# Cross-attention and a 4-bit-quantized FFN on one core: attention steps reordered, late scale guards, norm and splits re-placed

## The chip, the cores and the metric

The kernel runs on one core of a Trainium2 chip. A core has five engines that run their own instruction streams and meet through semaphores: PE (TensorE: matrix products and transposes), DVE (VectorE), ACT (ScalarE), POOL (GpSimd) and SP (SyncE, which here only issues DMAs). Times are device microseconds of one execution, the median of three runs for a kernel as a whole; the profile comes from one further execution. The granted clock is the share of full speed that PE was given.

## The reference

For 8 sequences of 128 rows of 512 values, cut to what is computed:

```python
x = x + xattn(layernorm(x), ctx, ctx, mask, Wq, Wk, Wv, Wo)
x = x + ffn(layernorm(x), w1, w2, w3)

# xattn: 32 query heads, 8 key/value heads of 128, rotary positions on q and k
logits = 30 * tanh(einsum(q, k) * 0.0884 / 30)
weights = softmax(where(mask, logits, -1e30))
attn = einsum(weights, v).reshape(b, t, 4096) @ Wo

# ffn: each of w1, w2 (1376 x 512), w3 (512 x 1376) goes through NF4:
# per 64 neighbours: absmax; w/absmax to the nearest of 16 codes; times absmax
h = silu(x @ dq1.T) * (x @ dq2.T)
out = h @ dq3.T
```

The mask is one 128 x 128 table for all sequences. The quantization of w1, w2, w3 is part of the computation.

## The kernel before

**Precision.** Each large product is taken as three PE products: both operands are split into a high half (rounded by an ACT copy) and a low half (source minus high, on DVE or POOL), and `product` adds high x low, high x high and low x high (L164 to L166). `split` is L150 and L151. So each product operand is preceded by an ACT instruction and a DVE or POOL instruction.

**Order.** The program switches on a manual schedule: each engine executes its instructions in the order in which the code issues them, and an instruction that must wait holds up all that is behind it on its engine. PSUM buffers are named by tags: "q" (two banks), "s" (one), "wo" (one), "pv" (two banks wide, one buffer), "c" (two banks wide, the quantizer's sum).

**Head** (first 118 us). A list of tiles, key, value and query projections, is walked; `plan[n]` holds what is to be issued beside tile n. `masks` turns the mask with PE (pm) and counts its valid keys with an all-ones product (pa). `scales` finds each block's absmax a, guards it against zero (r = max(a, 2^-126)) and inverts it, all on DVE. `Scales.turn` transposes a and r with PE (pt_ar), copies them out of PSUM on ACT (art, L310), and writes them to DRAM, from where they are read back broadcast (s_w).

**Quantizer.** `quantize` is a generator that goes through units of at most 128 x 1024 weights. A unit is multiplied by its inverse scales on POOL (w_w, L200), then 15 bounds follow, each an ACT instruction (nm_w, L190) and a DVE instruction (nc_w, L196, in PSUM), then it is multiplied by its scales and split by `store` (dqt or w3t). `pump(n)` advances it by about n bounds' worth; the calls of `pump` between other work set where quantization stands in the queues of ACT, DVE and POOL.

**Attention** (118 to about 600 us). 64 steps, one per (half of the batches x key/value head, batch). A step issues: `project` (output product of three steps ago, then acc += po on DVE), `store`, `turn` (transposes the attention output of two steps ago into aT, split by ACT and DVE), `end_store`, `pump`, `q_proj` (query product for the next unit of 4 steps, and the start of its rotation by `rope`: copies on ACT, rc_q on DVE, rs_q on POOL), `values` (weights x values of the last step, then 1/rowsum and ad on DVE), `scores` (logits pl on PE, tanh and exp on ACT, times mask on POOL), the rotation's last add (L447: on DVE for the first two units, on POOL later), and `pump`. `due` says in which step wo and wq weights are split.

**Norm and FFN.** From step 59 the second layer norm starts, two batches at a time: `LayerNorm.sums`, `finish` (1/sqrt by an integer guess and three refinements, `rsqrt`, L100 to L105, on DVE), `rows`. Then `gate_up` makes 22 pairs of products (pg, pu); a later call makes silu(pg) on ACT and hT = that x pu on DVE. `order` holds 20 of them, in a loop with `pump(3.45)`. The down product (pd) needs hT split into `hs` by `split_h`; three are split at the end of the loop, and one more in each iteration of the loop over `down`. Six batches' pd are kept in PSUM, batches 6 and 7 get theirs at the end.

## Time and profile before

| | |
|---|---|
| Median of three runs | 804.36 us (803.58 to 804.71) |
| Profiled execution | 806.1 us, its span 804.3 us |
| Mean granted clock | 0.994 |
| Busy: PE, DVE, ACT, POOL | 784.1, 640.2, 581.0, 462.0 us |
| PE waits over 2 us in all | po for acc 3.2 (3 times), po for aT 2.5 (twice), pd's first 2.4 (once) |
| DMA | 102.44 MB, mean 127 GB/s |

The span runs from the first to the last recorded instruction; the execution's own time has a little around it. Busy time counts an engine's instructions; PE's instructions overlap their neighbours slightly, so that a full PE reads as 97 to 100%. A wait row reads: engine, what waited, its line, what it waited for, then total, number and longest in us. Names are the program's with the numbers left out (po_17 is po).

### The profile page before, as it was taken

The numbers are of one execution on the slowest core, as the hardware profiler recorded it, in microseconds if no ns is written. First come the engines' busy times: TensorE is split into PE (matmuls) and PEld (weight loads), VectorE is DVE, ScalarE is ACT, GpSimd is POOL, SyncE is SP. The second block draws the span as 40 slices with busy tenths as digits, with TensorE's granted clock in tenths as the row PEclk, the third lists the DMA queues.
The fourth block names the chain that finished last, engine by engine and source line by source line (L and its number), as shares of the span: only waits on it lengthen the run. The fifth ranks groups of instructions, "written<-read, shape, count | busy, mean of one in ns | idle before, by whom it ended". The sixth has DMA issues, their size and how long they took to land.

```text
span 804.3 us, 11142 instructions
## 1 busy us (share of the span) xinstructions
PE 784.1 (97%) x3737; PEld 629.7 (78%) x3737; DVE 640.2 (80%) x875; ACT 581.0 (72%) x821; POOL 462.0 (57%) x370
## 2 busy tenths in 40 slices
PE   8899998999999999999999999999989999998998
PEld 6688876877877787787887878878768888886877
DVE  6747789889779797988898878888867788879941
ACT  6348767888887879798797979888522769759720
POOL 3469546687877778777787877877530322322100
PEclk9999999999999999999999999999999999998999
DMA  7856736435263616336164415330240335441011
GB/s 232 286 172 209 209 124 193 110 115 182 55 190 112 196 40 198 96 102 209 54 200 126 125 34 181 104 131 35 96 151 8 114 123 162 124 148 41 1 66 40
DMA packets 72167, 102.44 MB, mean 127 GB/s; under 512 B 6542, under 2 KB 41678, under 8 KB 72110
## 3 DMA queue, kind: packets, MB, share of 16 engines
q1 hardware_dynamic: 68942, 90.19, 36.3%
q0 software_dynamic: 3168, 11.54, 4.5%
q8 instruction: 30, 0.49, 0.3%
q14 instruction: 27, 0.22, 0.1%
HBM read 79.32 MB, written 22.38 MB: 126 GB/s over the span
## 4 chain that ended last, share of the span: by engine, by line
PE 82%; DVE 7%; issue 3%; DMA 3%; ACT 3%; POOL 1%; SPq 1%; DVEq 0%; POOLq 0%; ACTq 0%
PE po L166 7%; PE po L164 7%; PE po L165 7%; PE pq L164 7%; PE pq L166 6%; PE pq L165 6%; PE pv L659 6%; PE pl L646 6%; PE pt_a L157 3%; PE pd L166 3%; PE pd L164 3%; PE pd L165 3%; PE pvp L166 2%; PE pvp L164 2%; PE pvp L165 2%
## 5 line engine op out<-in xcount | busy, mean ns | idle before, releaser
L196 DVE SCALAR_TENSOR_TENSOR nc_w<-nm_w,nc_w 128x1024 f32<-128x1024 bf16 (+1 forms) x238 | 284.2, 1194 | 63.3 <-ACT nm_w L190 51.4
L190 ACT ACTIVATE nm_w<-w_w,bias 128x1024 bf16<-128x1024 f32 (+1 forms) x255 | 275.4, 1115 | 23.6 <-POOL w_w L200 19.2
L164 PE MATMUL po<-wo,aT 128*128 128x512 f32 x256 | 124.9, 488 | 3.2 <-DVE acc L673 3.2
L446 POOL TENSOR_TENSOR rs_q<-rs_q,sgnq 128x512 f32<-128x512 f32 x64 | 84.1, 1315 | 72.7 <-ACT rs_q L444 69.9
L652 POOL TENSOR_TENSOR th<-th,mt 128x512 f32<-128x512 f32 x64 | 83.6, 1306 | 43.0 <-ACT th L650 27.0
L164 PE MATMUL pq<-xT,wq 128*128 128x512 f32 x256 | 106.0, 414 | 0.3 <-DVE rc_q L445 0.3
L166 PE MATMUL po<-wo,aT 128*128 128x512 f32 x256 | 101.5, 397 | 2.5 <-DVE aT L151 2.5
L165 PE MATMUL po<-wo,aT 128*128 128x512 f32 x256 | 100.4, 392 | 0.0
L166 PE MATMUL pq<-xT,wq 128*128 128x512 f32 x256 | 100.2, 391 | 0.0
L165 PE MATMUL pq<-xT,wq 128*128 128x512 f32 x256 | 99.8, 390 | 0.0
L447 POOL TENSOR_TENSOR qr<-rc_q,rs_q 128x512 f32<-128x512 f32 x56 | 72.5, 1295 | 0.4 <-DVE rs L661 0.4
L659 PEld LDWEIGHTS pv<-vt,th 128*128 128x128 f32 x512 | 66.4, 191 | 4.9 <-POOL th L652 0.6
L164 PEld LDWEIGHTS po<-wo,aT 128*128 128x128 f32 x256 | 48.5, 190 | 27.4 <-issue 12.7
L659 PE MATMUL pv<-vt,th 128*128 128x129 f32 x512 | 67.6, 275 | 0.2 <-POOL th L652 0.2
L165 PEld LDWEIGHTS po<-wo,aT 128*128 128x128 f32 x256 | 48.7, 190 | 22.1 <-issue 13.8
L646 PE MATMUL pl<-qr,krt 128*128 128x512 f32 x128 | 65.6, 594 | 0.0
L443 ACT COPY rs_q<-pq 64x512 f32<-64x512 f32 x64 | 37.3, 582 | 38.9 <-PE pq L166 36.1
L200 POOL TENSOR_TENSOR w_w<-w_w,s_w 128x1024 f32<-128x1024 f32 (+1 forms) x17 | 39.8, 2343 | 43.1 <-DMA s_w<-scale_d 43.0
L649 ACT ACTIVATE th<-pl 128x512 f32<-128x512 f32 x64 | 38.4, 599 | 33.7 <-PE pl L646 33.2
L166 PEld LDWEIGHTS po<-wo,aT 128*128 128x128 f32 x256 | 48.4, 189 | 14.8 <-DVE aT L151 3.8
L166 PEld LDWEIGHTS pq<-xT,wq 128*128 128x128 f32 x256 | 48.0, 188 | 10.8
L164 PEld LDWEIGHTS pq<-xT,wq 128*128 128x128 f32 x256 | 48.2, 188 | 9.7 <-DVE rc_q L445 1.4
(141 smaller groups left out, 1710.0 us busy)
## 6 DMA issues: line engine op xcount, KB each, us to landing
s_w<-scale_d SPq DMA_DIRECT2D x60, 256.0 KB
w12t_d<-dqt SPq DMA_DIRECT2D x22, 512.0 KB
w<-w12t_d POOLq DMA_DIRECT2D x22, 512.0 KB, 4.5
raw_wq<-in_L_xattn_Wq SPq DMA_DIRECT2D x32, 256.0 KB
raw_wo<-in_L_xattn_Wo SPq DMA_DIRECT2D x32, 256.0 KB
ws<-in_L_ffn_w SPq DMA_DIRECT2D x20, 256.0 KB
w_w<-in_w12t SPq DMA_DIRECT2D x10, 512.0 KB
kr_d<-kr SPq DMA_DIRECT2D x16, 256.0 KB
```

The source lines that it names most:

```text
L164: E.matmul(out, ah, bl, start=start and i == 0, stop=False)
L165: E.matmul(out, ah, bh, start=False, stop=False)
L166: E.matmul(out, al, bh, start=False, stop=stop and i == n - 1)
L190: S.activation(m, self.w, AF.Relu, bias=bias[:self.p, i:i + 1], scale=BIG if up else -BIG)
L196: V.scalar_tensor_tensor(self.c, m, step, self.c, ALU.min, ALU.subtract if i == POS[0] else ALU.add)
L200: Q.tensor_tensor(self.w, self.w, self.s, ALU.mult)
L446: Q.tensor_tensor(s, s, every(sgn), ALU.mult)
L447: return lambda: (engine or Q).tensor_tensor(dst, c, s, ALU.add)
L646: E.matmul(pl, krt[kv, u % 2][:, bb * T:(bb + 1) * T], qr[u][:, bb].rearrange("p g t -> p (g t)"), start=True, stop=True)
L649: S.activation(th, pl, AF.Tanh, scale=ATTN_MULT / CAP)
L652: Q.tensor_tensor(em[i], em[i], mt.unsqueeze(1).to_broadcast([P, G, T]), ALU.mult)
L659: E.matmul(pv[:, g, :HD + 1], em[i][:, g], vt[kv][:, b], start=True, stop=True)
```

## The change

All parts keep the same arithmetic on the same data, and the same number of PE instructions (3,737 records before).

- `scales`: the guard goes from DVE to POOL, and the reciprocal becomes a later call: one tile later in the head, at the next bound in the quantizer. The scale turn is listed only after it. In the head, `store` begins at tile 9 instead of 6.
- `masks` is called at tile 6 and leaves its two PE steps and what hangs on them (`turn`, `count`) to tiles 10 and 12.
- Rotation: the second unit's last add goes to POOL; only the first unit's stays on DVE. With the new order it is issued before `values` and `scores` of its step, so ahead of that step's mask on POOL.
- Attention steps: the query product is issued first, then a pump (1.5; 1 in steps 0 and 1; none from 60), then projection, `turn` (step 2 no longer apart), then the rotation's last add, values, scores, and a pump of 1.65 instead of 2.15. One wo split moves from step 1 to step 2.
- Norm: for the first four batches the refinements of `finish` run on POOL, as four instructions each instead of three on DVE. The normalized rows 0 and 1 are made in step 61, rows 2 and 3 after the last step.
- Inner values: one split in each of the last four iterations of the gate_up loop instead of three in the last; the splits of batches 6 and 7 for the first two groups go to a separate buffer (`hs_67`), and are issued in the down loop from i = 2.
- Last banks: pd of batch 7 is made in two halves in different banks ("q" and "s"); before, both were halves of one bank.
- A small tile (`apart_2`) shifts addresses in the last pool.

```diff
...
 
-    def rsqrt(v, y, n, name):
+    def rsqrt(v, y, n, name, E=V):
         i = tp.tile([P, n], I32, tag="rs_i", name=f"i_{name}")
...
         for _ in range(3):
-            V.tensor_tensor(t, y, y, ALU.mult)
-            V.scalar_tensor_tensor(t, t, -0.5, v, ALU.mult, ALU.mult)
-            V.scalar_tensor_tensor(y, t, 1.5, y, ALU.add, ALU.mult)
+            E.tensor_tensor(t, y, y, ALU.mult)
+            if E is V:
+                E.scalar_tensor_tensor(t, t, -0.5, v, ALU.mult, ALU.mult)
+                E.scalar_tensor_tensor(y, t, 1.5, y, ALU.add, ALU.mult)
+            else:
+                E.tensor_tensor(t, t, v, ALU.mult)
+                E.tensor_scalar(t, t, -0.5, 1.5, ALU.mult, ALU.add)
+                E.tensor_tensor(y, y, t, ALU.mult)
 
...
 
-        def finish(self, apart=False):
+        def finish(self, engine=V, apart=False):
             n = len(self.bs)
...
             V.tensor_single_scalar(v, self.mv[:, :, 1], EPS, op=ALU.add)
-            rsqrt(v, self.y, n, self.name)
+            rsqrt(v, self.y, n, self.name, engine)
 
...
         V.tensor_reduce(a, blocks(w), AX.X, ALU.max, apply_absolute_value=True)
-        V.tensor_single_scalar(r, a, 2.0 ** -126, op=ALU.max)
-        V.reciprocal(r, r)
+        Q.tensor_single_scalar(r, a, 2.0 ** -126, op=ALU.max)
+        return lambda: V.reciprocal(r, r)
 
...
             self.s = nf.tile([P, 2, 16], F32, tag="nf_ar", name=f"ar_{self.h}")
-            scales(self.s[:, 0], self.s[:, 1], self.w)
-            fresh.append(self.turn)
+            last = scales(self.s[:, 0], self.s[:, 1], self.w)
+
+            def later():
+                last()
+                fresh.append(self.turn)
+            return later
 
...
             own = slice(self.cols.start // BLK, self.cols.stop // BLK)
-            scales(self.s[:, 0, own], self.s[:, 1, own], self.w)
-            if self.cols.stop == 4 * H:
-                fresh.append(self.turn)
+            last = scales(self.s[:, 0, own], self.s[:, 1, own], self.w)
+
+            def later():
+                last()
+                if self.cols.stop == 4 * H:
+                    fresh.append(self.turn)
+            return later
 
...
     def quantize():
+        invert = None
         for i, u in enumerate(units):
...
                 u.bound(b)
+                if invert:
+                    invert()
+                    invert = None
                 for when, s in found.get(i, ()):
...
                         yield 1
-                        s.find()
+                        invert = s.find()
                 if k == 2:
...
             product(pq, [((w[:, 0, k], w[:, 1, k]), (t[:, 0, k], t[:, 1, k])) for k in range(KT)])
-            return lambda: rope(qr[u][:, :, g, :], pq, cosq, sgnq, f"q{u}_{g}", V if u < 2 else None)
+            return lambda: rope(qr[u][:, :, g, :], pq, cosq, sgnq, f"q{u}_{g}", V if u < 1 else None)
 
...
                 Q.memset(ones, 1.0)
-                pm = bank("s", "pm")
-                E.transpose(pm[:, :T], mf, ident)
-                V.tensor_copy(mt, pm[:, :T])
-                pa = bank("s", "pa")
-                E.matmul(pa[:, :T], ones, mt, start=True, stop=True)
                 some = tp.tile([P, T], F32, tag="t_some", name="some", bufs=1)
-                V.tensor_single_scalar(some, pa[:, :T], 1.0, op=ALU.min)
-                V.tensor_tensor(cosq, tab[:, 0], some, ALU.mult)
-                V.tensor_tensor(sgnq, tab[:, 1], some, ALU.mult)
-                V.tensor_scalar(some, some, -1.0, 1.0, ALU.mult, ALU.add)
-                V.tensor_tensor(mt, mt, some, ALU.max)
+
+                def turn():
+                    pm = bank("s", "pm")
+                    E.transpose(pm[:, :T], mf, ident)
+                    V.tensor_copy(mt, pm[:, :T])
+
+                def count():
+                    pa = bank("s", "pa")
+                    E.matmul(pa[:, :T], ones, mt, start=True, stop=True)
+                    V.tensor_single_scalar(some, pa[:, :T], 1.0, op=ALU.min)
+                    V.tensor_tensor(cosq, tab[:, 0], some, ALU.mult)
+                    V.tensor_tensor(sgnq, tab[:, 1], some, ALU.mult)
+                    V.tensor_scalar(some, some, -1.0, 1.0, ALU.mult, ALU.add)
+                    V.tensor_tensor(mt, mt, some, ALU.max)
+                steps.extend([turn, count])
 
...
             plan[4] += [both[1].load]
-            plan[6] += [both[0].find]
-            plan[8] += [both[1].find]
+            inverts = []
+            plan[6] += [lambda: inverts.append(both[0].find())]
+            plan[7] += [lambda: inverts.pop()()]
+            plan[8] += [lambda: inverts.append(both[1].find())]
+            plan[9] += [lambda: inverts.pop()()]
             plan[12] += [units[0].load]
...
                 plan[20 + 2 * b].append(lambda b=b: turned[b]())
-            plan[8].append(masks)
+            steps = []
+            plan[6].append(masks)
+            plan[10].append(lambda: steps.pop(0)())
+            plan[12].append(lambda: steps.pop(0)())
             plan[15].append(lambda: ln.finish(apart=True))
...
                     f()
-                if 6 <= n < 19:
+                if 9 <= n < 19:
                     store()
...
 
-        due = {0: [("o", 0, 0)], 1: [("o", 0, 1), ("o", 0, 2), ("o", 0, 3)]}
+        due = {0: [("o", 0, 0)], 1: [("o", 0, 1), ("o", 0, 2)], 2: [("o", 0, 3)]}
         xn = {}
...
                 due.setdefault(i + (2 if i < 4 else 1), []).append(("q" if s8 < 4 else "o", kv + 1, s8 % 4))
+            tiles = {0: (0, 1), 1: (2,), 2: (3,), 3: ()}.get(i, (bb,)) if u + 1 < 2 * NKV else ()
+            later = [q_proj(u + 1, g) for g in tiles]
+            later = [f() for f in later]
+            pump(1.5 if 2 < i < 60 else 1 if i in (0, 1) else 0)
             if 0 <= i - 3:
...
                 ln.sums(i - 59)
+            if i == 61:
+                xn.update({k: pair.rows(k, "xn") for k in (0, 1)})
             store()
-            if 0 <= i - 2 and i > 2:
+            if 0 <= i - 2:
                 turn(i - 2)
             end_store()
-            if i < 60 and i != 2:
-                pump(1)
-            later = [q_proj(u + 1, g)() for g in ({0: (0, 1), 1: (2,), 2: (3,), 3: ()}.get(i, (bb,)))
-                      if u + 1 < 2 * NKV]
-            if i == 2:
-                turn(0)
+            for f in later:
+                f()
             if 0 <= i - 1:
...
             scores(i)
-            for f in later:
-                f()
-            pump(2.15 if 2 < i < 59 else 0)
+            pump(1.65 if 2 < i < 59 else 0)
             if i == 62:
...
             if i in (60, 62):
-                ln.finish()
-                xn.update({k: ln.rows(k, ("xn", "t2")[k // 2]) for k in (i - 60, i - 59)})
+                ln.finish(Q)
+                pair = ln
             for k in due.pop(i, ()):
...
 
+        xn.update({k: pair.rows(k, "t2") for k in (2, 3)})
         project(N - 3)
...
     f1 = ctx.enter_context(tc.tile_pool(name="f1", bufs=2))
+
+    f1.tile([P, 32], F32, name="apart_2", bufs=1)
     w3t, hs = {}, {}
 
+    last_hs, last_at = [(6, 0), (6, 1), (7, 0), (7, 1)], []
+
     def split_h(b, i):
         n = min(4, NHT - 4 * i)
-        t = hs[b, i] = wp.tile([P, 2, KT, P], F32R, tag="wq", name=f"hs_{b}_{i}", bufs=6)
+        if (b, i) in last_hs:
+            w = last_hs.index((b, i))
+            if not last_at:
+                last_at.append(wide("hs_67"))
+            t = hs[b, i] = last_at[0][:, :, :, w * P:(w + 1) * P]
+        else:
+            t = hs[b, i] = wp.tile([P, 2, KT, P], F32R, tag="wq", name=f"hs_{b}_{i}", bufs=6)
         split(t[:, 0, :n], t[:, 1, :n], hT[b // 4, i][:, :, b % 4 * T:b % 4 * T + T], V)
...
     down = most + [(b, 2) for b in range(6)] + [(b, i) for b in range(6, B) for i in range(3)]
-    to_split = list(down)
+    to_split = [k for k in down if k not in last_hs]
     last = len(order) - 1
...
             load_w12(w12_at[n])
-        if n == last:
-            for _ in range(3):
-                split_h(*to_split.pop(0))
+        if n >= last - 3:
+            split_h(*to_split.pop(0))
     evac()
...
             split_h(*to_split.pop(0))
+        if i == 2 and b < 4:
+            split_h(*last_hs[b])
         mine = pairs.setdefault(b, [])
...
             o = f1.tile([P, D], F32, tag="o", name=f"o_{b}", bufs=4)
-            if b >= 6:
-                pd.append(bank("q", f"pd_{b}"))
             parts = 2 if b == B - 1 else 1
...
                 own = slice(j * D // parts, (j + 1) * D // parts)
-                product(pd[b][:, own], [(s, (th[:, own], tl[:, own])) for s, (th, tl) in mine], start=b >= 6)
-                V.tensor_tensor(o[:, own], acc[b][:, own], pd[b][:, own], ALU.add)
+                to = pd[b] if b < 6 else bank(("q", "q", "s")[b - 6 + j], f"pd_{b}_{j}")
+                product(to[:, own], [(s, (th[:, own], tl[:, own])) for s, (th, tl) in mine], start=b >= 6)
+                V.tensor_tensor(o[:, own], acc[b][:, own], to[:, own], ALU.add)
                 nc.sync.dma_start(out[b][:, own], o[:, own])
```

## The prediction

> **What bounds the kernel now.** The profiled execution took 806.1 us with a span of 804.3; the runs' median is 804.36. I sum against the span and carry the difference over to the median unchanged. I read the page first, then PE's waits, then the waits in the timeline, then windows.
>
> ```profile
> PE 784.1 (97%) x3737; PEld 629.7 (78%) x3737; DVE 640.2 (80%) x875; ACT 581.0 (72%) x821; POOL 462.0 (57%) x370
> PE   8899998999999999999999999999989999998998
> PEclk9999999999999999999999999999999999998999
> PE 82%; DVE 7%; issue 3%; DMA 3%; ACT 3%; POOL 1%; SPq 1%; DVEq 0%; POOLq 0%; ACTq 0%
> ```
>
> PE is the bound: 97% busy, and 82% of the chain that ended last. From 250 to 350 us it is busy 100.00 of 100.00. There a step issues query product (12 matmuls at .227 us from start to start: 2.73), projection (2.73), four transposes (.44), eight value matmuls (.89) and logits (.86); that makes 7.65, and steps follow each other every 7.69. So no order of these can shorten a steady step: only PE's stalls and its low clock are to be had. I subtract those nominal spacings from the elapsed time: 34.5 us are lost in the whole span, 9.9 by 40 us, only 4.4 between 260 and 600 (2.3 to 573), and 10.1 after 730. The waits view names them:
>
> ```profile
> PE po L164 <- DVE acc L673: 3.2, 3, 1.5
> PE po L166 <- DVE aT L151: 2.5, 2, 1.7
> PE pd L164 <- issue: 2.4, 1, 2.4
> PE pd L166 <- DVE hs L151: 1.2, 1, 1.2
> PE pm L532 <- DVE mf L528: 0.9, 1, 0.9
> PE pt_ar L306 <- DVE ar L173: 0.7, 1, 0.7
> PE pa L535 <- DVE mt L533: 0.5, 1, 0.5
> PE pv L659 <- POOL th L652: 0.2, 1, 0.2
> ```
>
> (total, times, longest.) In windows (length, busy time of PE, PEld, DVE, ACT, POOL; then the granted clock) the clock follows a thin stretch:
>
> ```profile
> 130.40:133.90 3.50, 1.79 (x9) 0.87 (x7) 3.50 (x6) 2.52 (x5) 2.32 (x2) 1.00 0.69 209
> 581.00:584.40 3.40, 1.80 (x6) 0.57 (x6) 3.26 (x9) 1.23 (x2) 1.00 (x1) 1.00 0.00 0
> 584.40:587.80 3.40, 3.40 (x9) 2.62 (x10) 0.62 (x1) 0.00 (x0) 1.47 (x3) 0.51 0.50 139
> 731.20:734.60 3.40, 0.71 (x2) 0.30 (x2) 3.19 (x4) 3.40 (x6) 0.00 (x0) 1.00 0.27 88
> 734.60:738.00 3.40, 2.68 (x6) 2.15 (x7) 3.40 (x6) 3.40 (x6) 1.25 (x1) 0.50 0.07 28
> 738.00:741.40 3.40, 3.40 (x9) 2.64 (x8) 3.30 (x4) 2.98 (x4) 0.03 (x1) 0.50 0.11 36
> ```
>
> **1. Head, 30 to 37 us: -2.1 (-1.2 to -2.7).** The reciprocal moves one tile after its guard, the store of the first scale turn from tile 6 to 9, the mask's two PE steps to tiles 10 and 12. The waits of pt_ar, pm and pa (.7+.9+.5 in the view, 2.7 with the restarts in my account) lose their cause: their sources are then a tile (2.7 us) old. New: a scale turn lands directly after pm in the same bank and waits for a DVE copy, about .5. The two moved scale stores on SP stand just ahead of the loads that read them; a landing that is late there delays only the first quantization product on POOL. Late POOL work has about 3.5 us of slack here (the low halves of the last value weights end at 74.25 and are needed at 77.8).
>
> **2. Seam, steps 0 to 3: +3.5 (+1.5 to +5).** The final add of the second unit's rotated queries goes from DVE to POOL, ahead of step 0's mask; ACT gets one nm_w and one dqt copy ahead of step 0's tanh.
>
> ```profile
> 121.42 1.30 POOL L446 TENSOR_TENSOR rs_q<-rs_q,sgnq 128x512 f32<-128x512 f32 x1 [0.80 <-ACT rs_q L444]
> 122.72 1.71 POOL L652 TENSOR_TENSOR th<-th,mt 128x512 f32<-128x512 f32 x1
> 123.05 0.61 ACT L150 CAST dqt<-w_w 128x512 fp32r<-128x512 f32 x1
> 124.48 1.16 PE L659 MATMUL pv<-vt,th 128*128 128x129 f32 x8 [0.22 <-POOL th L652]
> ```
>
> Now the mask follows rs_q at once. In the new order POOL first has the dqt low half, which needs the ACT copy (ends near 123.1): 1.72 (its duration here), two adds and the mask at 1.30: 128.7, against 124.43. So the value matmuls, ready at 124.10, stall 4.65 instead of .38. PE's later stalls here (aT low half 1.92, .25, .27) have time to dissolve: 4.27-2.44 = +1.8. Then the clock. The Trainium skill, "TensorE: Matmul & The Clock Gate", Part 1, says that one idle window of about 3.4 us brings half clock; a 4.65 us stall covers a whole free-running window in (4.65-3.41)/3.41 = 36% of phases: .36 x 1.7 = +.6. The rows differ: 581.0 to 584.4 was only 1.6 idle, and the next window ran at .51; yet the similar 130.4 to 133.9 was not punished. A stall of 4.65 leaves some window with at least 2.3 idle, so I take one half-clock window, 3.4/2 = 1.7; ends 0 and 3.4.
>
> **3. Steady steps, 0 (±1), and the bubble at 246, -1.2.** Query product first, transposes directly before values, and pump shares 1.5/1.65 for 1/2.15: no PE work changes. acc, aT and ad get their readers later or at equal distance; laid out with the groups' mean durations, aT's low half ends 7.7 to 8.9 after its step's start and is due at 10.9, ad at 9.7 and is due at 13.15. The bubble is one event:
>
> ```profile
> 242.84 2.40 POOL L200 TENSOR_TENSOR w_w<-w_w,s_w 128x1024 f32<-128x1024 f32 x1
> 243.72 1.56 DVE L172 TENSOR_SCALAR ar<-ar 128x16 f32<-128x16 f32 x1
> 574.51 0.60 PE L157 MATMUL pt_a<-ident,ad 128*128 128x128 f32 x4
> 575.14 0.58 ACT L150 CAST aT<-pt_a 128x512 fp32r<-128x512 f32 x1 [1.94 <-PE pt_a L157]
> 575.88 1.12 PE L646 MATMUL pl<-qr,krt 128*128 128x512 f32 x2
> ```
>
> The scale guard, .17 to .45 elsewhere, took 1.56 on DVE until POOL's long product ended, acc came late and PE lost 1.25 in all. On POOL the guard can only queue behind that product, with nobody but the later reciprocal waiting. Its 17 pieces cost POOL at most .45 each, under cover of its 43% idle time.
>
> **4. A new wait, pl on the scale copy: +1.9 (+1.0 to +4.4).** In eight steps a scale turn uses bank "s" right before the attention transposes. The copy that frees the bank (L310, 249 ns mean) stands on ACT behind aT's high half. Before, the query product (2.73) lay between and covered it; now only four value matmul pairs do. From the last two PE rows pl is due 1.33 after pt_a's start once saturated (.44+.89). ACT: start .63, aT .58, copy .25, hand-over .1: 1.56. So .23 each is 1.9. Should an nm_w (1.1 us) or half of one stand ahead of it, .55 each: 4.4; low end .12.
>
> **5. Steps 59 to 63: -1.7 (-3.5 to +1.5).** Before: the two acc adds behind the norm chains on DVE (1.03, 1.67), aT low half .9, one half-clock window 1.7, rest .6: 5.9. Now three refinements run on POOL as 12 small operations. Nothing that small is on POOL here; two nearby rows, 1.30 for 512 columns and 2.40 for 1024, leave an intercept of .20, and I take .25: 3.0 us after step 60's mask (ends 579.67), so y at 582.7. The Trainium skill, "GPSIMD Engine Reference", section 3.1, counts an elementwise operation 1.96 times DVE's[...]: 1.96 x .20 (DVE's small ones start .20 apart) x 12 = 4.7. The normalized rows, moved to step 61, stand on DVE ahead of the next aT low half, so the projection stalls 2.3 by the row, 4.0 by the rule. I take the row; both ends are in the range. With .7 of a half-clock window (1.2) and .6: 4.1, so -1.8, rounded to -1.7.
>
> **6. Down stage, 715 to the end: -8.5 (-4 to -9.5).** Before, three splits of the inner values stand behind the last pump: PE waits 2.59 for the first high half (2.4 in the view), 1.37 for a low half, .36 more, and the next 6.08 busy us run at half clock, 3.04. Then 1.03 at 781 and .57 at 796, where the last bank is still read or its second half shares the bank: 8.96 in all. Splits at iterations 16 to 19, one each, last batches' splits from a buffer of their own, and separate banks take all of these away. New: the iterations shift quantization by one split (.6 ACT, 1.3 DVE), and the next unit's first product now comes in iteration 16; its scale loads landed up to 10.7 late (16.5 us waited at 705 to 745), which can make ACT's gate function late by about .35. -8.96+.35 = -8.6; I take -8.5. If that load is later, PE stalls at iteration 18 and half clock returns: -4.
>
> **Sum:** -2.1+3.5+0-1.2+1.9-1.7-8.5 = -8.1; 804.36-8.1 = **796.3 us**.
>
> **Rivals.**
> - *POOL's mask becomes the bound (slower).* The query add stands ahead of the mask in every step. Logits end at 7.70 of a step, tanh .60, exp .63, mask 1.30: 10.2; the next value matmuls are due at 7.69+5.9 = 13.6. If the query add waits so long behind DVE that the mask ends .14 past 13.6 in each of 57 steps, the 8.1 are gone; at .2 late, 11.4: about 808. For: POOL is 57% busy and 70 to 80% here. Against: 3.4 us of slack.
> - *Down gain halved.* Scale loads late, as in 6: 796.3+4.5 = 801. For: the 16.5 us wait; against: the unit's load is issued iterations earlier.
> - *No half clock at seam and transition.* 796.3-1.7-1.2-.9 (shorter finish) = 792.5. For: the unpunished 130.4 window; against: 4.65.
> - *The change doesn't do what it says:* the stalls only move to the next late work, as they would if DVE itself bounded; then within .2% of 804.4. Against: DVE 80% busy, idle in every steady step.
>
> **How the numbers follow.** Likeliest case .52 (794 to 799), Down halved .16, no half clock .12, nothing gained .07, POOL late .13. The range leaves out POOL late and some of both tails: 790.5 to 803.8. A time within .2% (1.6 us, what this measurement can tell) counts as the same. Faster: .52+.16+.12 = .80; same .07; slower .13.
>
> **What would show it.** Right: no PE wait on ar, mf, mt before 40 us; a wait of pv on POOL's th of 4 to 5 us near 122 to 127, with a lower clock in the slice after it; about eight short waits of pl on the ACT copy of art, .2 each; no PE gap near 246; po waiting some 2.3 on aT once near 581; the first down product straight after the last up product, full clock there, and no gaps in the last 25 us. Wrong: steps longer than 7.69 with pv waiting for POOL; PE waiting for a DVE product before a gate_up product after 715; a po wait over 4 us at 581.

## The result and the profile after

The changed kernel took 806.71 us (median of 16 runs, 804.49 to 807.97), the kernel before beside it 804.50 (803.15 to 806.53, 16 runs). The ratio is 1.0023, with a 95% interval of 1.0014 to 1.0033: some 1.9 us slower, by the ratio. The prediction said 796.3, with a range of 790.5 to 803.8. Both profiled executions have a span of 804.3 us; that of before was one of the slower executions of its kernel (806.1 us against 804.5), that of after about a middling one (806.12 against 806.71), so the traces show a difference of nothing where the medians show 2 us.

The page of the changed kernel, the same rows as shown of before (busy time, PE's tenths, the granted clock in tenths, the chain that ended last):

```profile
PE 783.5 (97%) x3737; PEld 631.3 (78%) x3737; DVE 627.2 (78%) x836; ACT 585.6 (73%) x821; POOL 473.3 (59%) x415
...
PE   8999996999999999999999999999989999998998
...
PEclk9999999999999999999999999999999999999999
...
PE 83%; ACT 4%; issue 4%; POOL 3%; DVE 3%; DMA 2%; SPq 1%; POOLq 0%; DVEq 0%; ACTq 0%
```

PE is still the bound. What differs is where it is idle: of the 40 slices the second has risen from 8 to 9, and the seventh (121 to 141 us) has fallen from 8 to 6. PE's waits (total, times, longest):

```profile
PE pv L687 <- POOL th L680: 5.0, 2, 4.8
PE po L171 <- DVE aT L156: 3.9, 2, 3.2
PE pg L169 <- ACT sg L747: 2.4, 1, 2.4
...
PE po L169 <- DVE wo L156: 1.2, 1, 1.2
...
PE pd L169 <- DVE o L885: 0.9, 1, 0.9
...
PE pt_ar L315 <- DVE mt L553: 0.4, 1, 0.4
```

The waits of before on ar, mf, mt and on the first hs are gone. In their place stand four others: the value matmuls on POOL's mask, the projection on aT, a gate product on silu, and the projection on the moved wo split. Windows around the three long ones (length, busy time of PE, PEld, DVE, ACT, POOL, then the clock, the DMA share and GB/s):

```profile
122.40:125.80 3.40, 0.00 (x0) 0.00 (x0) 2.12 (x2) 2.42 (x5) 3.40 (x3) 1.00 0.08 20
125.80:129.20 3.40, 2.73 (x9) 2.22 (x10) 1.79 (x3) 0.60 (x2) 3.40 (x4) 0.53 0.00 0
...
585.90:589.30 3.40, 0.77 (x3) 0.19 (x1) 2.09 (x3) 1.23 (x2) 2.60 (x7) 1.00 0.01 2
589.30:592.70 3.40, 2.85 (x7) 2.26 (x8) 1.27 (x3) 0.00 (x0) 0.84 (x2) 0.63 0.68 206
...
723.20:726.60 3.40, 1.29 (x6) 0.74 (x4) 0.74 (x1) 1.92 (x3) 1.45 (x1) 1.00 0.05 14
726.60:730.00 3.40, 3.11 (x7) 2.48 (x8) 3.30 (x5) 3.40 (x5) 0.00 (x0) 0.52 0.26 102
```

Each is followed by a window at about half clock; so each costs its wait and up to 1.7 us more (half of such a window).

**Where the time went.** As in the prediction I subtract PE's nominal spacings (.227 us for a 512-column matmul, and so on) from the elapsed time, and cut at the same places of PE's work, so that every kernel is cut alike. In the kernel before the stages are 11 to 50 us, 120 to 159, 159 to 569, 569 to 610, 704 to 730, and 730 to the end; of what is left out only the first 11 us lose more than .7, between 5.8 and 7.3. Lost us per stage in the profiled executions, of all kernels of this study (what each one changes stands in the next section):

```text
kernel         head  steps 0-3  other steps  steps 59-63  last gate_up   down
before         4.10     3.57        4.20         6.19         -0.04     10.11
changed        1.93     8.59        4.34         7.52          4.16      1.54
u1_phase       2.17     9.88        4.29         5.98          0.86      2.26
u2_rot         1.96     5.97        4.29         5.94          2.23      2.07
u3_norm        1.94     9.74        4.27         5.84          1.38      2.01
u4_art         1.91     9.69        2.75         7.46          2.93      2.06
u_seam         1.94     4.45        4.34         7.41          1.59      2.44
u_all          1.13     4.44        2.73         3.84          0.71      2.29
d_down         4.07     3.52        4.27         6.16          0.63      2.29
d_guard_down   1.93     3.55        2.72         4.61          0.61      2.42
d_order        4.06     9.83        5.71         5.83          1.81      9.34
d_no_order     1.95     3.57        2.77         7.46          1.22      2.76
n_rows         1.92     3.51        2.78         2.63          1.46      2.45
n_rows_last    1.43     3.56        2.74         2.62          1.14      1.66
```

Of after against before: head -2.2, steps 0 to 3 +5.0, other steps +.1, steps 59 to 63 +1.3, last gate_up iterations +4.2, down -8.6. Before rounding these sum to -.05, and the spans are equal. The down stage gave what was forecast; the gain was spent at two places before it, and half of it directly before it. The same code can show different sums in two executions: four kernels with the same steps 0 to 3 show 8.59, 9.69, 9.74 and 9.88, five in which every engine has the same instructions in the same order at steps 59 to 63 show 7.52, 7.46, 7.41, 5.98 and 5.94. In the latter the waits are the same to .02 (.89 and 3.34), and 8, 6, 6, 0 and 0 matmuls came at half rate after them: the stall is the same, and what the clock adds to it is not (the last section shows what decides it). So a part is read from its waits here, and from medians.

### The profile page after: what moved, and what is told of

Read it like the earlier page. It is cut to its first block, busy times and chain, and to the rows that moved or that the text cites. A ratio compares the mean times of both kernels' runs of the same rounds, so it can differ in the third digit from the quotient of the medians.

```text
span 804.3 us, 11078 instructions
## 1 busy us (share of the span) xinstructions
PE 783.5 (97%) x3737; PEld 631.3 (78%) x3737; DVE 627.2 (78%) x836; ACT 585.6 (73%) x821; POOL 473.3 (59%) x415
## 4 chain that ended last, share of the span: by engine, by line
PE 83%; ACT 4%; issue 4%; POOL 3%; DVE 3%; DMA 2%; SPq 1%; POOLq 0%; DVEq 0%; ACTq 0%
PE pq L169 7%; PE pq L171 7%; PE pq L170 7%; PE pv L687 6%; PE pl L674 6%; PE po L171 6%; PE po L169 6%; PE po L170 6%; PE pt_a L162 3%; PE pd L169 3%; PE pd L170 3%; PE pd L171 3%; PE pg L169 2%; PE pg L170 2%; PE pg L171 2%
## 5 line engine op out<-in xcount | busy, mean ns | idle before, releaser
L169 PE MATMUL pq<-xT,wq 128*128 128x512 f32 x256 | 124.1, 485 | 0.0
L171 PE MATMUL po<-wo,aT 128*128 128x512 f32 x256 | 101.1, 395 | 3.9 <-DVE aT L156 3.9
L169 PE MATMUL po<-wo,aT 128*128 128x512 f32 x256 | 102.1, 399 | 1.3 <-DVE wo L156 1.2
L170 PE MATMUL po<-wo,aT 128*128 128x512 f32 x256 | 100.7, 393 | 0.0
L171 PE MATMUL pq<-xT,wq 128*128 128x512 f32 x256 | 100.4, 392 | 0.0
L170 PE MATMUL pq<-xT,wq 128*128 128x512 f32 x256 | 100.1, 391 | 0.0
L464 POOL TENSOR_TENSOR qr<-rc_q,rs_q 128x512 f32<-128x512 f32 x60 | 77.8, 1297 | 2.6
L687 PEld LDWEIGHTS pv<-vt,th 128*128 128x128 f32 x512 | 63.0, 194 | 6.0 <-POOL th L680 6.0
L171 PEld LDWEIGHTS po<-wo,aT 128*128 128x128 f32 x256 | 48.5, 189 | 15.5 <-DVE aT L156 5.2
L462 DVE TENSOR_TENSOR rc_q<-pq,cosq 128x512 f32<-128x512 f32 x64 | 44.0, 687 | 21.1 <-ACT rs_q L461 19.2
L155 ACT CAST aT<-pt_a 128x512 fp32r<-128x512 f32 x64 | 36.9, 576 | 31.0 <-PE pt_a L162 31.0
L169 PEld LDWEIGHTS po<-wo,aT 128*128 128x128 f32 x256 | 48.4, 189 | 13.8 <-DVE wo L156 1.7
```

The source lines that it names most:

```text
L169: E.matmul(out, ah, bl, start=start and i == 0, stop=False)
L170: E.matmul(out, ah, bh, start=False, stop=False)
L171: E.matmul(out, al, bh, start=False, stop=stop and i == n - 1)
L462: V.tensor_tensor(c, src4, every(cos), ALU.mult)
L464: return lambda: (engine or Q).tensor_tensor(dst, c, s, ALU.add)
L687: E.matmul(pv[:, g, :HD + 1], em[i][:, g], vt[kv][:, b], start=True, stop=True)
```

## Experiments

Names that begin with u undo parts of the changed kernel; those with d do parts alone on the kernel before; n carries one part further. All compute the whole reference.

### u1_phase: one quantizer bound back

```diff
-pump(1.5 if 2 < i < 60 else 1 if i in (0, 1) else 0)
+pump(1.5 if 2 < i < 59 else 1 if i in (0, 1, 59) else 0)
```

> The changed kernel with step 59's pump at 1 instead of 1.5: one quantizer bound less ahead of the gate_up loop, so the next unit's first product falls behind the gate function of iteration 16 in ACT's order. Theory A (the late scale load holds the gate function only because one bound has moved ahead of it): the 2.4 us wait of pg on sg near 724 shrinks to at most .4 and the half-clock window after it goes: 3.8 us less than the changed kernel's 806.7, about 802.9. Theory B (the scale load is late whatever stands where): the wait moves one iteration on, pg waits 2 us or more near 729: 806 to 807.

Measured: 804.67 us, ratio to before 1.0000 (.9991 to 1.0009), so 1.9 us less than the changed kernel's 1.0023 (3.8 less was expected). First the wait in the changed kernel, in the timeline (start, duration; in brackets the idle time before and what ended it; ACT's, POOL's and PE's rows):

```profile
722.27 2.38 POOL L205 TENSOR_TENSOR w_w<-w_w,s_w 128x1024 f32<-128x1024 f32 x1 [11.62 <-DMA s_w<-scale_d]
724.68 1.15 ACT L195 ACTIVATE nm_w<-w_w,bias 128x1024 bf16<-128x1024 f32 x1 [10.60 <-POOL w_w L205]
725.74 0.60 ACT L155 CAST hs<-hT 128x512 fp32r<-128x512 f32 x1
726.25 0.59 ACT L747 ACTIVATE sg<-pg 128x512 f32<-128x512 f32 x1
...
726.89 0.79 PE L169 MATMUL pg<-xT,w 128*128 128x512 f32 x1 [2.40 <-ACT sg L747]
```

One nm_w of the next unit and the first inner-value split stand on ACT between two gate functions. That nm_w waits 10.6 us for the unit's scales to land, and the gate function, whose input had been ready for long, waits behind it; the gate bank is not free, and PE stops. In the kernel before, the product with the scales (POOL) and the first nm_w that waits for them (ACT) were:

```profile
717.04 2.39 POOL L200 TENSOR_TENSOR w_w<-w_w,s_w 128x1024 f32<-128x1024 f32 x1 [10.72 <-DMA s_w<-scale_d]
719.47 4.27 ACT L190 ACTIVATE nm_w<-w_w,bias 128x1024 bf16<-128x1024 f32 x4 [6.88 <-POOL w_w L200]
```

There ACT had made one more gate function, at 711.99, ahead of that nm_w, and PE did not wait. In u1_phase the same place:

```profile
715.02 0.60 ACT L155 CAST hs<-hT 128x512 fp32r<-128x512 f32 x1
716.60 0.60 ACT L747 ACTIVATE sg<-pg 128x512 f32<-128x512 f32 x1 [0.97 <-PE pg L171]
724.54 4.27 ACT L195 ACTIVATE nm_w<-w_w,bias 128x1024 bf16<-128x1024 f32 x4 [7.34 <-POOL w_w L205]
728.72 1.08 ACT L155 CAST w3t<-w_w 128x512 fp32r<-128x512 f32 x1
729.60 0.63 ACT L155 CAST hs<-hT 128x512 fp32r<-128x512 f32 x1
730.13 0.58 ACT L747 ACTIVATE sg<-pg 128x512 f32<-128x512 f32 x1
```

The scales landed just as late (POOL's product began at 722.12), but the gate function was ahead. The wait fell from 2.4 to .6 (expected: at most .4), the stage's loss from 4.16 to .86; the rest of the wait is one iteration on, where the added split (.6) stands before the next gate function. Theory A for the cause.

How much this order costs depends on when the load lands. Five traces have the changed kernel's order here. Counted from the same place of PE's work (704 us in the kernel before), with the losses of the table:

```text
kernel    product with the scales starts   pg waits   stage loses
u3_norm             12.53                    1.1         1.38
u_seam              12.72                    1.3         1.59
u2_rot              13.33                    1.9         2.23
changed             13.82                    2.4         4.16
u4_art              14.08                    2.7         2.93
```

The wait is in each the start less 11.4. Only the changed kernel's was followed by half clock, about 1.6 of its 4.16. In the seven traces with the order of u1_phase the product starts 13.1 to 14.0 after that place, and the stage loses .61 to 1.46. So the 3.3 us that the trace returns here are the upper end, which fits the 1.9 by which the median moved; besides, the profiled u1_phase lost 1.3 more in steps 0 to 3, where two windows of half clock followed instead of one.

### u2_rot and u_seam: steps 0 to 3

u2_rot puts the second unit's last rotation adds back on DVE:

```diff
-f"q{u}_{g}", V if u < 1 else None)
+f"q{u}_{g}", V if u < 2 else None)
```

> The changed kernel with the second unit's last rotation adds on DVE again. Theory A (POOL's queue ahead of step 0's mask makes the 4.8 us wait): pv waits under 1 us there, no half clock after it; of the 6.5 us lost between 120 and 130 some 5 come back, less what then waits for the last wo split (up to 2.5): 802.5 to 804.5. Theory B (ACT's nm_w and dqt ahead of tanh, or DVE, are as late as POOL): pv still waits 3 us or more: 806 to 807.

u_seam adds to it the wo split of step 1, and store and pump ahead of the query product in steps 0 and 1:

```diff
-        due = {0: [("o", 0, 0)], 1: [("o", 0, 1), ("o", 0, 2)], 2: [("o", 0, 3)]}
+        due = {0: [("o", 0, 0)], 1: [("o", 0, 1), ("o", 0, 2), ("o", 0, 3)]}
...
+            if i < 2:
+                store()
+                pump(1)
             tiles = {0: (0, 1), 1: (2,), 2: (3,), 3: ()}.get(i, (bb,)) if u + 1 < 2 * NKV else ()
...
-            pump(1.5 if 2 < i < 60 else 1 if i in (0, 1) else 0)
+            pump(1.5 if 2 < i < 60 else 0)
...
-            store()
+            if i >= 2:
+                store()
```

> The changed kernel with rotation adds on DVE, the wo split back in step 1, and in steps 0 and 1 store and pump ahead of the query product as before. Theory A (after the rotation adds, the remaining 2.4 us wait of pv comes from nm_w and dqt standing ahead of tanh on ACT and so of the mask on POOL, and po's 1.0 from the moved wo split): both go, the loss between 120 and 157 us falls from 6.0 to 4 or less, about 799.5. Theory B (the new order in itself starves the mask): pv still waits over 1.5 us: 801 to 802.

Measured: u2_rot 801.58 us, ratio .9959 (.9944 to .9973); u_seam 801.29, ratio .9958 (.9944 to .9972). In the changed kernel POOL's queue here reads:

```profile
119.33 1.29 POOL L463 TENSOR_TENSOR rs_q<-rs_q,sgnq 128x512 f32<-128x512 f32 x1 [1.62 <-ACT rs_q L461]
121.02 1.28 POOL L156 TENSOR_TENSOR dqt<-w_w,dqt 128x512 fp32r<-128x512 f32 x1 [0.39 <-ACT dqt L155]
122.25 2.94 POOL L464 TENSOR_TENSOR qr<-rc_q,rs_q 128x512 f32<-128x512 f32 x2
125.15 1.27 POOL L680 TENSOR_TENSOR th<-th,mt 128x512 f32<-128x512 f32 x1
```

The mask follows two adds and a low half, without a pause. PE's waits of u2_rot, then those of u_seam:

```profile
PE pv L687 <- POOL th L680: 2.5, 2, 2.4
...
PE pg L169 <- ACT sg L747: 1.9, 1, 1.9
...
PE po L169 <- DVE wo L156: 1.0, 1, 1.0
```

```profile
PE pt_a L162 <- DVE ad L690: 1.4, 1, 1.4
...
PE pv L687 <- POOL th L680: 0.3, 2, 0.2
```

The two adds (2.94 us on POOL) were 2.4 of the 4.8 us that pv waits. The other 2.4 came from nm_w and dqt ahead of tanh on ACT, and the low half of dqt ahead of the mask on POOL: with them moved, .2 is left, and the wait on wo is gone too (which of the two instructions weighs more was not tried). A new one of 1.4, of the transposes on ad, takes part of it. So u2_rot came out between its theories (pv waits 2.4, where A had less than 1 and B 3 or more): POOL's queue made one half of the wait, what stood ahead of tanh and the mask the other. For the second half u_seam shows its theory A; its stage loss, 4.45, is a little over the expected 4, and its time is not the 799.5 that was expected. Its median does not show the 1.5 us that the stage gained over u2_rot: the profiled u_seam lost 1.5 more at steps 59 to 63, where its code is the same and 6 matmuls came at half rate against none.

### u3_norm: the refinements back on DVE

```diff
-            if i == 61:
-                xn.update({k: pair.rows(k, "xn") for k in (0, 1)})
...
-                ln.finish(Q)
-                pair = ln
+                ln.finish()
+                xn.update({k: ln.rows(k, ("xn", "t2")[k // 2]) for k in (i - 60, i - 59)})
...
-        xn.update({k: pair.rows(k, "t2") for k in (2, 3)})
```

> The changed kernel with the refinements on DVE and the normalized rows where they were before. Theory A (the rows standing on DVE behind POOL's chain make the 3.2 us wait of po on aT): that wait goes, two waits of 1 to 1.7 on acc return, and 1.3 us are gained: 805.4. Theory B (with transposes and values drawn together the acc add is late in either case): 807 or more.

Measured: 804.35 us, ratio .9994 (.9986 to 1.0002), 2.3 us less than the changed kernel. The trace does not give the credit to one place: the stage loses 5.84, hardly less than the 5.94 to 5.98 of two other executions with the changed kernel's stage; PE waits 1.5 in two pieces on aT, and 1.5 and .9 ahead of the first matmul of two projections, in sum about the .9 and 3.2 that they replace, but in smaller pieces, and none was followed by half clock. The wait of pg at the end was 1.1 instead of 2.4 (nothing there was changed). Inconclusive alone; d_no_order and n_rows settle this part.

### u4_art: the scale turn ahead of the projection

```diff
+            store()
             if 0 <= i - 3:
                 project(i - 3)
...
-            store()
+            end_store()
             if 0 <= i - 2:
                 turn(i - 2)
-            end_store()
```

> The changed kernel with the scale turn issued ahead of the projection and its copy ahead of the transposes' high half on ACT. Theory A (pl waits for that copy in eight steps): the eight losses of .17 to .42 us in those steps go, 1.5 to 2 us less: 805. Theory B (they come from elsewhere, such as the pumps): the steps keep their losses: 806.7.

Measured: 806.01 us, ratio 1.0016 (1.0005 to 1.0027), which alone does not tell it from the changed kernel. The traces do: between 175 and 510 us the changed kernel's first logits product comes late at seven places, at 218.3, 257.0, 303.5, 342.2, 388.6, 435.0 and 497.0, which are seven of the eight scale turns, by .2 to .3 us each. u4_art has none of these delays, and the loss of these steps falls from 4.34 to 2.75. Theory A: 1.6 us. The median fell by only about .6, less than the intervals can tell.

### d_order: the attention part alone on the kernel before

```diff
-f"q{u}_{g}", V if u < 2 else None)
+f"q{u}_{g}", V if u < 1 else None)
...
-        due = {0: [("o", 0, 0)], 1: [("o", 0, 1), ("o", 0, 2), ("o", 0, 3)]}
+        due = {0: [("o", 0, 0)], 1: [("o", 0, 1), ("o", 0, 2)], 2: [("o", 0, 3)]}
...
+            later = [q_proj(u + 1, g) for g in tiles]
+            later = [f() for f in later]
+            pump(1.5 if 2 < i < 60 else 1 if i in (0, 1) else 0)
             if 0 <= i - 3:
                 project(i - 3)
...
-            pump(2.15 if 2 < i < 59 else 0)
+            pump(1.65 if 2 < i < 59 else 0)
```

> The kernel before with the attention part alone: query product first, rotation adds, pumps and the wo split as in the changed kernel. Theory A (this part is a pure cost): 5 to 6 us more at steps 0 to 3, 1.6 in the steps with a scale turn, steps 59 to 63 and the end within 1 of before: 811 to 813. Theory B (it costs only together with the others): within 2 us of 805.

Measured: 815.15 us, ratio 1.0136 (1.0122 to 1.0149), 10.9 us slower than before. Its waits:

```profile
PE pv L659 <- POOL th L652: 4.8, 1, 4.8
...
PE pg L164 <- ACT sg L719: 1.6, 1, 1.6
...
PE po L164 <- DVE wo L151: 1.3, 1, 1.3
PE pl L646 <- ACT art L340: 1.0, 1, 1.0
```

Theory A, and more than expected: steps 0 to 3 cost 6.3, the scale turns 1.5 (one wait of pl on the art copy, 1.0, is long enough to be listed by itself), and the extra quantizer bound 1.85 at the last gate_up iterations, though no split of inner values is there. Outside steps 0 to 3 and the scale turns it had been expected to stay within 1 us; it took 2 us more than the 813 expected at most. It is the part that makes the change slower.

### d_down, d_guard_down, d_no_order: the other parts

d_down has the change's lines from `f1` to the end on the kernel before, in the main:

```diff
-    to_split = list(down)
+    to_split = [k for k in down if k not in last_hs]
...
-        if n == last:
-            for _ in range(3):
-                split_h(*to_split.pop(0))
+        if n >= last - 3:
+            split_h(*to_split.pop(0))
...
+        if i == 2 and b < 4:
+            split_h(*last_hs[b])
...
+                to = pd[b] if b < 6 else bank(("q", "q", "s")[b - 6 + j], f"pd_{b}_{j}")
```

The buffer `hs_67` is as in the change. d_guard_down adds the guards, the masks and the head's plan:

```diff
-        V.tensor_single_scalar(r, a, 2.0 ** -126, op=ALU.max)
-        V.reciprocal(r, r)
+        Q.tensor_single_scalar(r, a, 2.0 ** -126, op=ALU.max)
+        return lambda: V.reciprocal(r, r)
...
-                if 6 <= n < 19:
+                if 9 <= n < 19:
```

and d_no_order adds the norm's part, and so is everything but the attention part:

```diff
+            if i == 61:
+                xn.update({k: pair.rows(k, "xn") for k in (0, 1)})
...
-                ln.finish()
+                ln.finish(Q)
+                pair = ln
```

> The kernel before with the Down part alone (splits of the inner values, their buffer, the last banks). Theory A (the part is worth what its waits cost, where no quantizer bound has moved): the 10.1 us lost after 730 fall to 2 to 3: 797 to 798 against 805. Theory B (the late scale load takes the gain back here too): a wait of pg or pd of 2 us or more with half clock, 800 to 803.

> The kernel before with the Down part and the guards on POOL with their later reciprocals, stores and mask steps. Theory A: 3.3 us less than the Down part alone (2.1 in the head, 1.2 at the bubble near 246): 794 to 795. Theory B (guards on POOL cost later, where a reciprocal waits behind POOL's long product): nothing or less beyond the head's 2.1.

> Everything but the attention part: guards, norm on POOL with the rows one step later, Down part. Theory A (the norm's part is worth 1.7 us, as step 5 of the prediction has it, once the transposes and values are not drawn together): 792 to 793. Theory B (it is worth nothing or costs up to 1.5 in any order): 795 to 797.

Measured: d_down 798.14 us, ratio .9923 (.9910 to .9937); d_guard_down 795.42, .9885 (.9872 to .9899); d_no_order 797.27, .9912 (.9899 to .9926), all against 804.65 of before.

- The Down part alone is worth 6.2 us by the ratio, theory A. Its stage loss falls from 10.11 to 2.29, while .63 goes to the gate stage (pg waits .4), where the first split and the late scales meet even without an extra bound.
- The guards add 3.1 us by the ratios (3.3 expected). The stage table gives 2.1 in the head and 1.5 in the steps (4.27 to 2.72): the bubble at 246 is gone. Two reciprocals do wait on POOL's guard, .7 us each, but PE waits for nothing that is listed between 160 and 560 us. Theory A.
- The norm's part costs 2 us in this company too: theory B, a little over its 1.5. Part of this is the clock: two of d_guard_down's four executions ran at full clock throughout (794.20 and 794.59 us, against 796.25 and 796.51), none of d_no_order's did. Its waits are the changed kernel's 3.2 of po on aT and 1.7 more:

```profile
PE po L171 <- DVE aT L156: 4.9, 2, 3.2
```

### n_rows: the rows behind the low half

On d_no_order:

```diff
-            if i == 61:
-                xn.update({k: pair.rows(k, "xn") for k in (0, 1)})
             store()
             if 0 <= i - 2 and i > 2:
                 turn(i - 2)
             end_store()
+            if i == 61:
+                xn.update({k: pair.rows(k, "xn") for k in (0, 1)})
```

> Everything but the attention part, with the two normalized rows of step 61 issued behind the transposes' low half on DVE instead of ahead of it. Theory A (the rows' place, behind POOL's chain and ahead of that low half, is what makes the norm's part cost 1.9 us): po's 3.2 us wait on aT goes, the loss at steps 59 to 63 falls from 7.5 to 4.5 or less, about 794. Theory B (POOL's chain itself is too long): the wait moves to the acc add or the transposes of the rows, 796 to 798.

Measured: 793.43 us, ratio .9861 (.9842 to .9881), some 4 us less than d_no_order and 2 less than d_guard_down (whose interval it just overlaps). The stage of steps 59 to 63 loses 2.63 instead of 7.46. In the changed kernel DVE's and PE's rows at that place are (the first line is of the kernel before):

```profile
581.09 1.00 DVE L145 TENSOR_SCALAR xn_y<-acc,mv_y,y_y 128x512 f32<-128x512 f32 x2
...
587.21 1.98 DVE L150 TENSOR_SCALAR xn_y<-acc,mv_y,y_y 128x512 f32<-128x512 f32 x2 [1.52 <-POOL y_y L110]
589.12 0.68 DVE L156 TENSOR_TENSOR aT<-pt_a,aT 128x512 fp32r<-128x512 f32 x1
...
589.85 0.51 PE L171 MATMUL po<-wo,aT 128*128 128x512 f32 x1 [3.18 <-DVE aT L156]
```

and in n_rows the low half is ahead of them:

```profile
578.47 0.66 DVE L156 TENSOR_TENSOR aT<-pt_a,aT 128x512 fp32r<-128x512 f32 x1
...
580.02 2.07 DVE L150 TENSOR_SCALAR xn_y<-acc,mv_y,y_y 128x512 f32<-128x512 f32 x2 [0.89 <-POOL y_y L110]
```

DVE sits idle for POOL's last refinement in both; only in the first does PE's next operand stand behind that. Theory A.

### u_all: the changed kernel with all repairs

u_seam, with step 59's pump at 1, the scale turn ahead of the projection (u4_art) and the rows of step 61 behind the low half.

> The changed kernel with all repairs: steps 0 to 3 as in the run before, step 59's pump at 1, scale turn ahead of the projection, rows behind the low half. Theory A (query product first costs nothing once its side effects are undone): 794 to 796, as everything but the attention part. Theory B (it has a cost of its own): 798 or more.

Measured: 793.97 us, ratio .9873 (.9857 to .9888); the ratios of d_guard_down and n_rows lie in that interval. PE waits 2.6 on ad and 1.9 on aT in all, .2 on the mask and .4 on silu. Theory A: query product first has no price of its own, and no gain over the other order that these runs could tell.

### n_rows_last: the wait at 781

```diff
-    down = most + [(b, 2) for b in range(6)] + [(b, i) for b in range(6, B) for i in range(3)]
+    down = most + [(b, 2) for b in (4, 0, 1, 2, 3, 5)] + [(b, i) for b in range(6, B) for i in range(3)]
```

> The kernel with everything but the attention part and the late rows, and batch 4's last down products taken ahead of those of batches 0 to 3 and 5. Theory A (PE's .9 us wait on o near 781 is batch 5's product waiting until batch 4's sum has been read from the two-bank tile that both share): the wait goes, 1.0 us less: 792.4. Theory B (it is batch 6's product waiting for a bank of tag q): the wait stays, 793.4.

Measured: 791.63 us, ratio .9836 (.9817 to .9854), the fastest of all, 13 us below before (its interval overlaps that of n_rows, so the step is read from the trace). Its list of PE's waits holds none on o any more; what is left of the end:

```profile
PE pd L169 <- POOL w3t L156: 1.0, 1, 1.0
PE pg L169 <- ACT sg L747: 0.8, 1, 0.8
```

Theory A: batch 5's last products waited until batch 4's sum had been read out of the other half of the tile that both share; the down stage's loss fell from 2.45 to 1.66.

## Why the prediction was wrong

By its steps, against the profile and the runs:

1. **Head, -2.1: right.** -2.2 in the trace; the new wait of pt_ar on the DVE copy is .4 (taken: .5).
2. **Steps 0 to 3, +3.5: the stall right, the rest too low.** pv waited 4.81 (4.65). Of the 2.44 of later stalls that were to dissolve, the moved wo split brought 1.4 back (1.2 of wait and the restart), a wait that the step had not seen, although the split stood in the diff. Half clock followed, as taken. In the trace +5.0, in other executions of this code, with two half-clock windows instead of one, +6.1 to +6.3: above the upper end of 5. Of the two ways to weigh the clock, the fully idle window (122.40 to 125.80) was followed by half clock, as the Trainium skill ("TensorE: Matmul & The Clock Gate", Part 1) says of an idle window, so at this place its rule and the row came out alike (a stall of 4.65 leaves over 2 us of some window idle wherever the boundaries of the last section fall). Elsewhere the row is the better guide: the window from 586.8, in which PE had .24 us of work, and that of the kernel before from 581.0, with 1.40, were not wholly idle and were followed by half clock too (last section); there the measurement goes further than the page.
3. **Steady steps, 0, and the bubble, -1.2: right.** With step 4's waits gone, the steps lose 2.75 (u4_art), 1.45 less than before.
4. **pl on the scale copy, +1.9: right**, at 1.6 (u4_art): seven places at .23 each, where it had eight at .23.
5. **Steps 59 to 63, -1.7: wrong in sign.** The wait of po on aT was 3.2 instead of 2.3 and another of .9 came on aT two steps earlier; half clock followed in some executions, as its .7 allowed. POOL's twelve operations took 3.24 us (583.95 to 587.18), .27 each: near the row's .25, not the .39 of the estimate from the Trainium skill ("GPSIMD Engine Reference", 3.1), whose 1.96 stands there for 2,048 columns. The failed term is what stands behind them: the two rows took 1.98 where they took 1.00 before, running beside POOL's mask (why they were slower was not tried), and the low half started only at 589.12. d_no_order shows +2 us against d_guard_down for this part, n_rows that it is the rows' place and not POOL's chain: some 2 less than d_guard_down with them behind the low half (the intervals just overlap), against the -1.7 that the step had.
6. **Down stage, -8.5: the gain right, its new price wrong; this is the step that failed by most.** The down stage lost 8.57 less. But "which can make ACT's gate function late by about .35" was 4.2 in the trace: 2.56 of wait and 1.6 of half clock; the five traces with this order lose 1.4 to 4.2 here, and the median of u1_phase gives 1.9 for it. The next unit's first product had been seen to come into iteration 16, and its scales were taken to land in time for all but .35. Seen from PE's own position they were .9 later than before (POOL's product starts 13.82 us after the place at 704 in the kernel before, before it was 12.96): about as late as ever. But before, a gate function with its free bank stood ahead of the instruction that waits for them, and now behind it, so the lag falls on PE. u1_phase, with the one bound put back, shows it. This was the rival "Down gain halved": it had -4.0 for the end, and the trace has -4.4, but the time did not come down to its 801, since steps 2 and 5 failed too.
7. The wait at 781, which step 6 counted to the gain, stayed (.9): it belonged to the tile shared by batches 4 and 5 and not to the last banks (n_rows_last).

So three terms failed, in the prediction's own order: the later stalls of step 2, the sign of step 5, and the .35 of step 6. One reading of its overview is off as well: it has 4.4 us lost between 260 and 600, where the trace has 8.1 (the table's 6.19 for steps 59 to 63 lie within); no term rests on it.

Summed by the trace: -2.2 (head) +5.0 +.1 (steps) +1.3 -4.4 (the end, both stages), before rounding -.05, where the prediction had -8.1: 3.0 are missing at the transition, 1.5 at steps 0 to 3, 4.1 at the end, and -.6 stand the other way in the steps. The medians add 2 us to that, since the profiled execution of before was 1.6 us above its median and that of after .6 below. By whole runs the change is two: the attention part costs 10.9 us alone, all the rest gains 7.1 alone. Their sum, 3.8, is 1.9 more than the two cost together; where they overlap was not traced.

## What to carry to other kernels

In an in-order queue, count not only which instructions move but what each one waits for: an instruction that waits 10 us for a load is harmless at the end of its group and costs PE its stall, at times with half clock on top, if one instruction of PE's chain falls behind it; so half a unit of pump credit decided 2 us of the median here, and 3 in the trace. Before a move is priced at "nothing else changes", list for every engine what now stands ahead of the next operand of the bound engine, its waits included: two adds and a low half made one of the four new stalls, two row products another, a moved split a third, an early bound the fourth. And test a change of many parts by its parts: one part cost more than all others gained.

## What the runs showed of the hardware that was not expected

Whether a thin stretch is followed by half clock is not settled by its length alone: the same two waits (.89 and 3.34 us, the same to .02 in five executions) were followed by 8, 6, 6, 0 and 0 half-rate matmuls. This is worth up to 1.6 us per place, of the order of the effects measured here, so single traces of a stage differ by as much.

What settles it can be worked out from the fourteen traces. In each, the granted clock changes only at multiples of 3.413 us from its first change, as if time were cut into windows of that length; where the boundaries fall differs from trace to trace. For every such window I add up PE's work in it, by the nominal spacings. Windows from the long wait on (start, PE's work in it):

```text
kernel     window           next window        half clock after it
changed    586.78   .24                         yes
u4_art     585.81   .19                         yes
u_seam     583.03   .23                         yes
u1_phase   586.63  1.65     590.05  1.71        no
u2_rot     582.33  1.81     585.74  1.54        no
```

Where the 3.34 us fell into one window, half clock followed for the next; where a boundary divided them, it did not. From 12 us on, all windows of all traces fit: of those at full clock, the 21 with at most 1.40 us of work were each followed by a half-clock window, and none of the 3,173 with 1.42 or more. Only 5 of the 21 were without any work. (In the first 12 us three windows with 1.36 went without; the warming products there do not keep the nominal spacings.) The two windows that the prediction found alike, from 581.0 and from 130.4 in the kernel before, have 1.40 and 1.55 on this count. What is not shown is the limit for other kinds of PE work, or on other programs. So a stall that leaves PE more than about 2.0 us of a window idle is at risk, and whether it pays is a matter of where the boundaries fall.
